# A state-space scan on one Trainium2 core: the skip term as a diagonal product in the sum over states, and the gate applied on VectorE

## The chip, the cores and the metric

The kernel runs on one core of one Trainium2 chip. The metric is the device time of one execution in microseconds; before the change it is 18559.42 us, the median of three runs (18539.3 to 18562.05).

## What is computed

Two layers over an image of 8 x 128 x 128 x 128 (batch, channels, height, width), both added to their input. The first is an attention layer in frequency and space; the change doesn't touch it. The second is a selective state-space layer (Mamba). Per batch the 16,384 pixels are a sequence of vectors of 128 channels; `W_in` makes 256 inner channels `xs` and 256 gate channels `z`. Cut to what matters:

```python
xc = silu(conv(xs))                       # 4 taps along the sequence
dt, Bm, Cm = split(xc @ W_xproj)          # 16 states
delta = softplus(dt @ W_dt + b_dt)
h = exp(delta * A) * h + (delta * xc) * Bm      # per step, inner channel and state
y = sum over states of h * Cm
y = y + xc * D_param                      # the skip term
y = y * silu(z)                           # the gate
out = y @ W_out
```

All of it is float32.

## The kernel before

The second layer is the scan part, the last section of `tile_kernel`. It takes the sequence in chunks of T = 512 pixels: 32 chunks for each of 8 batches, 256 cycles in all. The state space of a chunk has 256 inner channels x 16 states = 4,096 rows of 512 pixels. One step works on 2 x 128 of these rows, so a chunk has ST = 16 steps. Step s of chunk i does, each on its own engine:

- `product` (L1239, TensorE): delta * xc times Bm for the 256 rows, as 32 small products with diagonal matrices (`bd`), into the PSUM tile `hb` (two banks, two such tiles in turn). In the profile it is a run of 64 records `hb<-bd,duT`. It is issued one step ahead of its scan.
- `decay` (L1231, ScalarE): exp(delta * A), two tiles `dA`, three steps ahead.
- `scan` (L1254, VectorE): two `tensor_tensor_scan` instructions of 128x512 that run the recurrence along the pixels, `hs<-dA,state,hb`.
- `keep_state` (ScalarE): the last column, kept for the next chunk.
- `weigh` (L1268, GpSimd): times Cm, 128x1024, into `hc`.
- `add` (L1273, TensorE): the sum over states. Group g is the four steps 4g to 4g+3; each of their tiles is multiplied by `gath` (four identity matrices of 32 on top of each other), 32 output rows a product, and summed in the PSUM tile `y`. Groups 0 and 1 make the half h = 0 of the 256 channels, groups 2 and 3 the half h = 1. A product shows as two records.

Around these stands the work of once a chunk, spread over the steps by hand in the list `beside` (L1319): an entry (step, which chunk, function) says at which step it is issued, and for the chunk before (-1), this one (0), the next (1) or the one after (2). The convolution (`conv`, products `e_xc`), `gate` (`e_z`, then silu into `sz`), `xproj` (`e_x`), `step_sizes` (`e_dt`, then softplus into `dl`), `drive` (delta * xc), `turn` (transposes `e_t`), `diagonals` (the tiles `bd`, VectorE), `project` (the product with W_out, `e_o`) and `residual` are such entries. Each engine's instructions go through `InOrder` (L169), which keeps them in the order in which they are written: in step n `keep_state(n-1)`, `product(n+1)`, `first`, `decay(n+3)`, `scan(n)`, `beside`, `weigh(n)`.

The PSUM tiles are: two `hb` of two banks each, and four single banks, one tag each (`bank`, L1091). `y` has bank 3 to itself.

What the change touches is the end of a chunk's sum. `add(i, 0, ...)` in steps 5 and 6 and `add(i, 1, ...)` in step 10 sum the half h = 0; in step 11 `skip(i, 0)` (L1288) adds xc * D on VectorE, reading `y` from PSUM and writing `yt` in SBUF; in step 12 `gated(i, 0)` (L1297) multiplies `yt` by `sz` in place on GpSimd. The half h = 1 follows with `add(i, 2, ...)` in step 14, and in the next chunk `add(i, 3, ...)` in step 2, `skip` in step 3 and `gated` in step 4. `project` reads both halves of `yt` in step 8. `xc` is made by `conv_act` (L1105) in step 2 for the next chunk, in three buffers.

```python
dve.scalar_tensor_tensor(
    c["yt"][:, h, :], c["xc"][:, h, :], d_par[:, h : h + 1], c.pop(("y", h)), ALU.mult, ALU.add
)
```

Of the kernel before, what the change touches and what calls it, by code (L numbers as in the profile page):

```python
# [9 lines left out]
F32 = mybir.dt.float32  # L10
AF = mybir.ActivationFunctionType
ALU = mybir.AluOpType
# [15 lines left out]
T = 512  # L28
# [162 lines left out]
def tile_kernel(ctx: ExitStack, tc: tile.TileContext, I: dict, out: bass.AP):  # L191
    nc = tc.nc
# [23 lines left out]
    i = _CONSTS.index("group4")  # L216
# [48 lines left out]
    with tc.tile_pool(name="a_x", bufs=12) as xp_, tc.tile_pool(name="a_p", bufs=5) as pp_, tc.tile_pool(  # L265
        name="a_t", bufs=2
    ) as tp_, tc.tile_pool(name="a_s", bufs=2) as sp_, tc.tile_pool(name="a_ps", bufs=3, space=PSUM) as psum, tc.tile_pool(
        name="a_pg", bufs=2, space=PSUM
    ) as psumg:
        pe, dve, act, gps = (InOrder(tc, e) for e in (nc.tensor, nc.vector, nc.scalar, nc.gpsimd))  # L270
# [150 lines left out]
    with tc.tile_pool(name="b_x", bufs=1) as xp_, tc.tile_pool(name="b_g", bufs=2) as gp_, tc.tile_pool(  # L421
        name="b_w", bufs=2
    ) as wk, tc.tile_pool(name="b_s", bufs=1) as sp_, tc.tile_pool(name="b_ps", bufs=8, space=PSUM) as psum:
        pe, dve, act, gps = (InOrder(tc, e) for e in (nc.tensor, nc.vector, nc.scalar, nc.gpsimd))
# [21 lines left out]
        def bank(name):  # L446
            return psum.tile([128, 512], F32, name=name, tag="ps")
# [175 lines left out]
        def gated(n):  # L623
            b, g = divmod(n, NGR)
            qt, c0 = g // 4, 4 * (g % 4)
            e, o = (t.rearrange("p (c s) -> p c s", c=4) for t in live.pop(("x", n)))
            d = live["d", b, qt][:, c0 : c0 + 4, 1:64]
            out_, tmp = (wk.tile([128, 2, 4, 128], F32, name=n_, bufs=k) for n_, k in (("eo", 2), ("et", 1)))
            for j, t in enumerate((e, o)):
                a0 = live["g", b, qt, j][:, c0, 0:1]  # L630
                a = bass.AP(a0.tensor, a0.offset, [a0.ap[0], [NU, 4], [1, 2], [1, 64]])
                dve.tensor_tensor(
                    out_[:, j].rearrange("p c (t s) -> p c t s", t=2), t.rearrange("p c (t s) -> p c t s", t=2), a, ALU.mult
                )
            cs, sn = slice(1, 64), slice(64, 127)
            for to, at, frm, by in ((0, cs, o[:, :, sn], half), (0, sn, o[:, :, cs], mhalf),
                                    (1, cs, e[:, :, sn], mhalf), (1, sn, e[:, :, cs], half)):
                dve.scalar_tensor_tensor(tmp[:, to, :, at], d, by, frm, ALU.mult, ALU.mult)
            mid = [t.rearrange("p j c s -> p (j c) s")[:, :, 1:127] for t in (out_, tmp)]
            gps.tensor_tensor(mid[0], mid[0], mid[1], ALU.add)  # L640
            live["p", n] = out_
# [43 lines left out]
        for n in range(total + 3):  # L685
            b, g = divmod(n, NGR)
            if 0 <= n - 1 < total:
                fft_x(n - 1)
                gated(n - 1)
# [43 lines left out]
    with tc.tile_pool(name="c_w", bufs=1) as cw_, tc.tile_pool(name="c_qk", bufs=1) as qkp, tc.tile_pool(  # L733
        name="c_x", bufs=4
    ) as srcp, tc.tile_pool(name="c_v", bufs=8) as vp_, tc.tile_pool(name="c_s", bufs=2) as sp_, tc.tile_pool(
        name="c_ps", bufs=6, space=PSUM
# [8 lines left out]
        pe, dve, act, gps = (InOrder(tc, e) for e in (nc.tensor, nc.vector, nc.scalar, nc.gpsimd))  # L745
# [15 lines left out]
        def conv(n, o, r):  # L761

            b, cv, gq = order[n]
            if o == 0:
                banks[n, r] = psum.tile([128, 2, 256], F32, name="c_mm", tag="ps")
            grid = ahead[n].rearrange("p f (i j) -> p f i j", j=GR)
            rs = slice(32 * r, 32 * r + 32)
            for s in range(4):
                y0, x0 = 8 * s + o // 2, o % 2
                pe.matmul(  # L770
                    banks[n, r][32 * s : 32 * s + 32].rearrange("p f (i j) -> p f i j", j=32),
                    lhsT=taps[rs, gq, cv, o, :], rhs=grid[rs, :, y0 : y0 + 8, x0 : x0 + 32],
                    start=(o == 0), stop=(o == 3),
                )
            if o == 3:
                (use_q, use_k, use_v, use_v)[cv](b, cv, 4 * gq + r, banks.pop((n, r)))
                if r == 3:
                    ahead.pop(n)
                    load(n + 4)
# [107 lines left out]
    with tc.tile_pool(name="d_o", bufs=1) as op_, tc.tile_pool(name="d_v", bufs=2) as vp_, tc.tile_pool(  # L887
        name="d_k", bufs=2
    ) as kp, tc.tile_pool(
        name="d_w", bufs=3  # L890
    ) as wk, tc.tile_pool(name="d_s", bufs=1) as sp_, tc.tile_pool(name="d_pa", bufs=2, space=PSUM) as psa, tc.tile_pool(
        name="d_ps", bufs=4, space=PSUM
    ) as psum:
        pe, dve, act, gps = (InOrder(tc, e) for e in (nc.tensor, nc.vector, nc.scalar, nc.gpsimd))
# [130 lines left out]
    with tc.tile_pool(name="e_c", bufs=1) as cp, tc.tile_pool(name="e_w", bufs=2) as wk, tc.tile_pool(  # L1025
        name="e_h", bufs=4
    ) as hp, tc.tile_pool(name="e_d", bufs=3, space=DRAM) as dp, tc.tile_pool(
        name="e_b", bufs=2, space=PSUM
    ) as hbp, tc.tile_pool(name="e_g", bufs=1, space=PSUM) as psum:
        def fixed(name, shape, src):  # L1030
            t = cp.tile(shape, F32, name=name)
            nc.sync.dma_start(t if len(shape) == 2 else t.rearrange("p a b -> p (a b)"), src)
            return t
# [3 lines left out]
        unit = fixed("unit", [128, 128], I["consts"][:, 0:128])  # L1037
# [3 lines left out]
        wout = fixed("wout", [128, 2, C], I["wout"])  # L1041
        dv = fixed("dv", [128, 6], I["dvec"])
        conv_b, b_dt, d_par = dv[:, 0:2], dv[:, 2:4], dv[:, 4:6]
        A = fixed("A", [128, NM, NBK], I["alog"])
        nc.scalar.activation(A, A, AF.Exp)
        nc.vector.tensor_scalar(A, A, -1.0, None, ALU.mult)  # L1046

# [5 lines left out]
        ch = {}  # L1053
# [4 lines left out]
        pe, dve, act, gps = (InOrder(tc, e) for e in (nc.tensor, nc.vector, nc.scalar, nc.gpsimd))  # L1058
# [45 lines left out]

        def conv_act(i):  # L1105
            c = ch[i]
            c["xc"] = wk.tile([128, 2, T], F32, name="xc", bufs=3)
            for h in range(2):
                act.activation(c["xc"][:, h, :], c.pop(("xcp", h)), AF.Silu, bias=conv_b[:, h : h + 1])

# [68 lines left out]
        def turn_act(i, part):  # L1179
            c = ch[i]  # L1180
            if part == 0:
                c["duT"] = wk.tile([128, NTB, DI], F32, name="duT")
            act.copy(c["duT"][:, 2 * part : 2 * part + 2, :].rearrange("p j d -> p (j d)"), c.pop("tp"))
# [14 lines left out]
        def diagonals(i, mp, j):  # L1198


            c = ch[i]
            if (mp, j) in ((0, 0), (1, 0)):
                c["bd", mp] = wk.tile([128, NTB, NQ, ND, 2], F32, name="bd")
            to = [128, NQ, ND, 2]
            b = c["bp"][:, 32 * j : 32 * j + DS].rearrange("p (q m) -> p q m", m=NM)[:, :, 2 * mp : 2 * mp + 2]
            dve.tensor_tensor(
                c["bd", mp][:, j], same.unsqueeze(1).unsqueeze(3).to_broadcast(to), b.unsqueeze(2).to_broadcast(to), ALU.mult
            )
# [22 lines left out]
        def decay(n):  # L1231
            i, h, mp, k = where(n)
            for j in range(2):
                dA = hp.tile([128, T], F32, name="dA", bufs=10)
                kk = 4 * h + k
                act.activation(dA, ch[i]["dlr", h][:, k, :], AF.Exp, scale=A[:, 2 * mp + j, kk : kk + 1])
                dAs[n, j] = dA
# [35 lines left out]
        def add(i, g, *js):  # L1273

            if g % 2 == 0 and 0 in js:
                ch[i]["y", g // 2] = bank("y", 3)
            for j in js:
                for k in range(4):
                    pe.matmul(
                        ch[i]["y", g // 2][k * NR : (k + 1) * NR, :], lhsT=gath, rhs=hcs[ST * i + 4 * g + k][:, j, :],  # L1280
                        start=(g % 2 == 0 and j == 0), stop=(g % 2 == 1 and j == 1), skip_group_check=True,
                    )
            if 1 in js:
                for k in range(4):
                    del hcs[ST * i + 4 * g + k]


        def skip(i, h):  # L1288

            c = ch[i]  # L1290
            if h == 0:
                c["yt"] = wk.tile([128, 2, T], F32, name="yt", bufs=1)
            dve.scalar_tensor_tensor(
                c["yt"][:, h, :], c["xc"][:, h, :], d_par[:, h : h + 1], c.pop(("y", h)), ALU.mult, ALU.add
            )

        def gated(i, h):  # L1297
            yt = ch[i]["yt"][:, h, :]
            gps.tensor_tensor(yt, yt, ch[i]["sz"][:, h, :], ALU.mult)

        def project(i):
            c = ch[i]
# [4 lines left out]
        def residual(i):  # L1307
# [15 lines left out]
            (1, 1, lambda i: conv(i, 1, 3)),  # L1323
            (1, 0, lambda i: more_diagonals(i, range(11, 16))),
            (2, 1, conv_act),
            (2, -1, lambda i: add(i, 3, 0, 1)),
            (3, -1, lambda i: skip(i, 1)),
            (4, -1, lambda i: gated(i, 1)),
            (4, 1, xproj),
            (5, 1, xproj_act),  # L1330
            (5, 0, lambda i: add(i, 0, 0)),
            (6, 0, lambda i: add(i, 0, 1)),
            (6, 1, step_sizes),
            (6, 2, norm),
# [5 lines left out]
            (9, 1, lambda i: drive(i, 1)),  # L1340
            (9, 2, lambda i: conv(i, 0, 0)),
            (10, 0, lambda i: add(i, 1, 0, 1)),
            (11, 0, lambda i: skip(i, 0)),
            (11, 1, lambda i: diagonals(i, 0, 0)),
            (11, 1, lambda i: turn(i, 0)),
            (11, 2, lambda i: conv(i, 0, 1)),
            (12, 0, lambda i: gated(i, 0)),
            (12, 1, lambda i: turn_act(i, 0)),
            (12, 1, lambda i: diagonals(i, 0, 1)),
            (12, 2, lambda i: conv(i, 0, 2)),  # L1350
# [15 lines left out]
        for n in range(-2 * ST, (total + 1) * ST):  # L1366
            i, s = divmod(n, ST)
# [40 lines left out]
```

## Time and profile before

| what | value |
|---|---|
| median of three runs | 18559.42 us |
| the profiled execution | 18481.4 us, its span 18479.6 us |
| scan part | from about 6,600 us to the end |
| scans `hs`, VectorE | 7936 + 256, 1,269 and 1,206 ns each |
| products `hb`, TensorE | 262144 records, 4919.3 us busy |
| sum over states `y`, TensorE | 16384 records, 2053.4 us busy |
| `e_x`, `e_z`, `e_o`, TensorE | 1024 records each, 517.4, 522.6 and 509.5 us busy |
| `hc`, GpSimd | 4096, 2,377 ns each |
| skip, `yt<-xc,dv,y`, VectorE | 512, 731 ns each |
| gate, `yt<-yt,sz`, GpSimd | 512, about 1,279 ns each |

The times of a group of instructions are the union of its instructions (busy) and the mean length of one; lengths on TensorE overlap, since a product starts before the one ahead of it has left the array, so the distance between two starts tells more of its price than its length. In a timeline a row is a run of like instructions: start, length, engine, line, operation, output<-inputs, shapes, number of records, and in brackets the idle time of that engine before it with what ended it. Line L180 is the helper of `InOrder` through which nearly all instructions pass, so the tiles' names tell them apart.

### The profile page before, as it was taken

The page shows a single profiled execution, that of the slowest core. Times are in us where ns is not written, and L with a number is a line of the kernel's source. Part 1 is how long each engine was busy: PE and PEld are TensorE (multiplying, and loading weights), DVE is VectorE, ACT ScalarE, POOL GpSimd, SP SyncE. Part 2 cuts the span into 40 slices and gives each one's busy share as a digit, 9 for nine tenths or more (in the row PEclk, how much of TensorE's full clock was granted, in tenths as well). Part 3 has the DMA queues.
Part 4 walks back from the last instruction along what each step waited for, and adds up shares of the span by engine and source line. Part 5 has one row for each costly group of instructions (what it writes and reads, how often), then busy time and mean ns, then how long its engine had stood idle before and what let it go on. Part 6 is the DMA issues. An engine that isn't in the chain of part 4 may idle for free.

```text
span 18479.6 us, 790974 instructions
## 1 busy us (share of the span) xinstructions
PE 16503.3 (89%) x353336; PEld 9529.9 (52%) x353336; DVE 14244.2 (77%) x15987; ACT 12009.6 (65%) x26077; POOL 13090.9 (71%) x7572
## 2 busy tenths in 40 slices
PE   7789988888888889999999999999999999999998
PEld 5566665566555544444444444444444444444444
DVE  5544544334444479999999999999999999999999
ACT  4443434334233358778778878888888878887887
POOL 3333334444222269999999999999999989998998
PEclk8889999988999999999999999999999999999999
DMA  9963337777776654444454445444544454445443
GB/s 375 371 235 89 96 106 248 240 230 218 207 204 192 186 139 100 103 96 100 97 105 101 100 96 108 99 99 98 106 98 99 100 103 100 99 98 105 98 98 88
DMA packets 2434566, 2601.34 MB, mean 141 GB/s; under 512 B 1221965, under 2 KB 1624013, under 8 KB 2396866
## 3 DMA queue, kind: packets, MB, share of 16 engines
q1 hardware_dynamic: 1730850, 2206.28, 43.9%
q10 hardware_dynamic: 679840, 277.32, 7.1%
q0 software_dynamic: 20480, 67.13, 1.1%
q8 instruction: 2783, 45.60, 1.1%
q14 instruction: 613, 5.02, 0.1%
HBM read 1715.23 MB, written 834.93 MB: 138 GB/s over the span
## 4 chain that ended last, share of the span: by engine, by line
PE 56%; DVE 22%; DMA 8%; issue 7%; ACT 6%; POOL 1%; SPq 1%; DVEq 0%; ACTq 0%; POOLq 0%
DVE hs L180 15%; PE hb L180 14%; PE y L180 8%; PE c_mm L180 6%; PE e_xc L180 4%; DVE bd L180 3%; PE e_z L180 3%; PE e_x L180 3%; PE d_b L180 2%; PE a_mm L180 2%; DMA d_of<-OFL 2%; PE c_gram L180 2%; PE d_p L180 2%; DMA X<-d_x 2%; ACT L180 2%
## 5 line engine op out<-in xcount | busy, mean ns | idle before, releaser
L180 POOL TENSOR_TENSOR hc<-hs,crep 128x1024 f32<-128x1024 f32 x4096 | 9653.4, 2377 | 982.4 <-DVE hs L180 858.1
L180 DVE TENSOR_TENSOR_SCAN hs<-dA,state,hb 128x512 f32<-128x512 f32 x7936 | 9611.4, 1269 | 558.2 <-PE hb L180 418.8
L180 PEld LDWEIGHTS hb<-bd,duT 64*32 64x32 f32 x262144 | 3727.5, 106 | 3971.3 <-issue 2808.4
L180 PE MATMUL hb<-bd,duT 64*32 64x128 f32 x262144 | 4919.3, 275 | 798.9 <-issue 417.8
L180 ACT ACTIVATE dA<-dlrep,A 128x512 f32<-128x512 f32 x8192 | 5443.8, 714 | 59.6 <-DMA dlrep<-dld 51.6
L180 PE MATMUL e_xc<-u,wf 128*128 128x512 f32 x4096 | 2263.9, 646 | 34.1 <-DVE A L1046 20.8
L180 PE MATMUL y<-hc,gath 128*32 128x512 f32 x16384 | 2053.4, 601 | 32.5 <-issue 31.2
L180 ACT COPY state<-hs 128x2 f32<-128x2 f32 x4096 | 775.9, 189 | 1676.2 <-DVE hs L180 1649.5
L180 ACT ACT_TABLE_LOAD x1057 | 1356.1, 1283 | 75.0 <-PE e_dt L180 40.1
L180 PE MATMUL c_mm<-src,taps 32*32 32x512 f32 x32768 | 1211.5, 626 | 191.8 <-issue 158.7
L180 DVE COPY vst<-c_mm 128x512 f32<-128x512 f32 x1024 | 685.0, 689 | 717.4 <-PE c_mm L180 620.6
L180 ACT ACTIVATE bd<-same,bt 128x64 f32<-128x64 f32 x4096 | 1054.0, 339 | 0.8 <-PE hb L180 0.8
L180 DVE TENSOR_TENSOR bd<-same,e_bt 128x512 f32<-128x512 f32 x1536 | 1036.7, 675 | 0.0
L180 PEld LDWEIGHTS c_mm<-src,taps 32*32 32x32 f32 x32768 | 681.2, 105 | 683.7 <-issue 493.5
L180 POOL TENSOR_SCALAR qm<-vst,cst 128x512 f32<-128x512 f32 x256 | 505.4, 2070 | 745.4 <-DVE vst L180 745.2
L180 ACT ACTIVATE junk<-vst 128x256 f32<-128x256 f32 x1024 | 416.4, 410 | 923.0 <-DVE vst L180 921.9
L180 PE MATMUL a_mm<-xt,wp 128*128 128x256 f32 x3072 | 760.6, 409 | 264.5 <-ACT pk L180 184.1
L180 POOL TENSOR_TENSOR eo<-eo,et 128x1008 f32<-128x1008 f32 x128 | 298.8, 2334 | 969.3 <-DVE et L180 960.8
L180 POOL DMA_DIRECT2D X<-d_x x256 | 139.1, 543 | 1069.5 <-DVE d_x L180 939.9
L180 PEld LDWEIGHTS e_xc<-u,wf 128*128 128x128 f32 x4096 | 654.7, 194 | 440.2 <-issue 436.1
L180 DVE TENSOR_TENSOR d_x<-d_p,d_x 128x512 f32<-128x512 f32 x256 | 274.9, 1074 | 780.3 <-DMA d_x<-in_x 490.0
L180 PEld LDWEIGHTS a_mm<-xt,wp 128*128 128x128 f32 x3072 | 619.3, 205 | 421.7 <-ACT pk L180 194.6
(179 smaller groups left out, 20011.2 us busy)
## 6 DMA issues: line engine op xcount, KB each, us to landing
dlrep<-dld SPq DMA_DIRECT2D x2048, 256.0 KB
crep<-cd SPq DMA_DIRECT2D x2048, 128.0 KB
dld<-dl SPq DMA_DIRECT2D x256, 512.0 KB
src<-Pq SPq DMA_DIRECT2D x128, 544.5 KB
src<-Pv SPq DMA_DIRECT2D x128, 544.5 KB
src<-Pk SPq DMA_DIRECT2D x128, 544.5 KB
src<-Px SPq DMA_DIRECT2D x128, 544.5 KB
xt<-in_x SPq DMA_DIRECT2D x64, 1024.0 KB
```

The lines of the kernel that those rows point to most:

```text
L180: made = method(*args, **kwargs)
```

## The change

A matrix `dd` is made once: for each half a 128 x 128 diagonal matrix of D_param (VectorE multiplies the identity `unit` by the column of D). Where `add` takes a new bank for `y` (g = 0 in step 5, g = 2 in step 14), a product of `dd` with `xc` now opens the sum (`start=True`), 128 x 128 by 128 x 512 in float32; the products with `gath` all add to it. `skip` is gone. `gated` moves from GpSimd to VectorE and to `skip`'s places, steps 11 and 3: a `tensor_tensor` that multiplies `y`, read from PSUM, by `sz` into `yt`. `xc` has two buffers instead of three.

```diff
--- before.py
+++ after.py
@@ -1041,6 +1041,9 @@
         wout = fixed("wout", [128, 2, C], I["wout"])
         dv = fixed("dv", [128, 6], I["dvec"])
         conv_b, b_dt, d_par = dv[:, 0:2], dv[:, 2:4], dv[:, 4:6]
+        dd = cp.tile([128, 2, 128], F32, name="dd")
+        for h in range(2):
+            nc.vector.tensor_scalar(dd[:, h, :], unit, d_par[:, h : h + 1], None, ALU.mult)
         A = fixed("A", [128, NM, NBK], I["alog"])
         nc.scalar.activation(A, A, AF.Exp)
         nc.vector.tensor_scalar(A, A, -1.0, None, ALU.mult)
@@ -1104,7 +1107,7 @@
 
         def conv_act(i):
             c = ch[i]
-            c["xc"] = wk.tile([128, 2, T], F32, name="xc", bufs=3)
+            c["xc"] = wk.tile([128, 2, T], F32, name="xc", bufs=2)
             for h in range(2):
                 act.activation(c["xc"][:, h, :], c.pop(("xcp", h)), AF.Silu, bias=conv_b[:, h : h + 1])
 
@@ -1274,29 +1277,24 @@
 
             if g % 2 == 0 and 0 in js:
                 ch[i]["y", g // 2] = bank("y", 3)
+                pe.matmul(ch[i]["y", g // 2], lhsT=dd[:, g // 2, :], rhs=ch[i]["xc"][:, g // 2, :], start=True, stop=False, skip_group_check=True)
             for j in js:
                 for k in range(4):
                     pe.matmul(
                         ch[i]["y", g // 2][k * NR : (k + 1) * NR, :], lhsT=gath, rhs=hcs[ST * i + 4 * g + k][:, j, :],
-                        start=(g % 2 == 0 and j == 0), stop=(g % 2 == 1 and j == 1), skip_group_check=True,
+                        start=False, stop=(g % 2 == 1 and j == 1), skip_group_check=True,
                     )
             if 1 in js:
                 for k in range(4):
                     del hcs[ST * i + 4 * g + k]
 
 
-        def skip(i, h):
+        def gated(i, h):
 
             c = ch[i]
             if h == 0:
                 c["yt"] = wk.tile([128, 2, T], F32, name="yt", bufs=1)
-            dve.scalar_tensor_tensor(
-                c["yt"][:, h, :], c["xc"][:, h, :], d_par[:, h : h + 1], c.pop(("y", h)), ALU.mult, ALU.add
-            )
-
-        def gated(i, h):
-            yt = ch[i]["yt"][:, h, :]
-            gps.tensor_tensor(yt, yt, ch[i]["sz"][:, h, :], ALU.mult)
+            dve.tensor_tensor(c["yt"][:, h, :], c.pop(("y", h)), c["sz"][:, h, :], ALU.mult)
 
         def project(i):
             c = ch[i]
@@ -1324,8 +1322,7 @@
             (1, 0, lambda i: more_diagonals(i, range(11, 16))),
             (2, 1, conv_act),
             (2, -1, lambda i: add(i, 3, 0, 1)),
-            (3, -1, lambda i: skip(i, 1)),
-            (4, -1, lambda i: gated(i, 1)),
+            (3, -1, lambda i: gated(i, 1)),
             (4, 1, xproj),
             (5, 1, xproj_act),
             (5, 0, lambda i: add(i, 0, 0)),
@@ -1340,11 +1337,10 @@
             (9, 1, lambda i: drive(i, 1)),
             (9, 2, lambda i: conv(i, 0, 0)),
             (10, 0, lambda i: add(i, 1, 0, 1)),
-            (11, 0, lambda i: skip(i, 0)),
+            (11, 0, lambda i: gated(i, 0)),
             (11, 1, lambda i: diagonals(i, 0, 0)),
             (11, 1, lambda i: turn(i, 0)),
             (11, 2, lambda i: conv(i, 0, 1)),
-            (12, 0, lambda i: gated(i, 0)),
             (12, 1, lambda i: turn_act(i, 0)),
             (12, 1, lambda i: diagonals(i, 0, 1)),
             (12, 2, lambda i: conv(i, 0, 2)),
```

## The prediction

> **What bounds the kernel now.** I read the page's shares first, then the table of waits, then the engines' timelines over one cycle. The scan part runs from about 6,600 us to the end, in 256 cycles of 16 steps (32 scans each). From 8,000 to 18,300 us the groups hold 6901 + 224 scans, that is 222.6 cycles in 10,300 us: **46.3 us a cycle**. Page, part 1:
>
> ```profile
> PE 16503.3 (89%) x353336; PEld 9529.9 (52%) x353336; DVE 14244.2 (77%) x15987; ACT 12009.6 (65%) x26077; POOL 13090.9 (71%) x7572
> ```
>
> Over the whole span no engine looks full. In the scan part alone six windows of 1,000 us give VectorE 949, TensorE 920 and GpSimd 918 us of busy time per 1,000. Busy time can't choose between them; who waits for whom can. From the waits of 8,000 to 18,300 us (engine and tile, releaser: us in total, times, longest):
>
> ```profile
> DVE hs L180 <- PE hb L180: 388.2, 532, 4.5
> ...
> PE hb L180 <- issue: 372.4, 258, 4.4
> PE hb L180 <- DVE hs L180: 300.7, 470, 1.2
> ...
> DVE hs L180 <- POOL hc L180: 31.1, 48, 2.6
> ...
> DVE yt L180 <- PE y L180: 9.0, 7, 2.8
> ```
>
> The two engines hold each other: VectorE's scan waits for TensorE's product hb 388.2 us (1.74 a cycle), and TensorE waits for a scan to free one of the two hb buffers 300.7 us (1.35 a cycle). GpSimd holds the scan up for 0.14 us a cycle. So the question is where in the cycle each wait stands. VectorE in a cycle without disturbance (start, length, what, idle before):
>
> ```profile
> 9785.41 4.80 DVE L180 TENSOR_TENSOR_SCAN hs<-dA,state,hb 128x512 f32<-128x512 f32 x4 [0.55 <-PE hb L180]
> 9790.63 2.45 DVE L180 TENSOR_TENSOR_SCAN hs<-dA,state,hb 128x512 f32<-128x512 f32 x2 [0.43 <-PE hb L180]
> ...
> 9817.15 7.14 DVE L180 TENSOR_TENSOR_SCAN hs<-dA,state,hb 128x512 f32<-128x512 f32 x6
> 9824.20 0.73 DVE L180 SCALAR_TENSOR_TENSOR yt<-xc,dv,y 128x512 f32<-128x512 f32 x1
> ...
> 9830.00 2.45 DVE L180 TENSOR_TENSOR_SCAN hs<-dA,state,hb 128x512 f32<-128x512 f32 x2 [0.36 <-PE hb L180]
> ```
>
> I find the steps by what stands between the scans: the scans of steps 6 and 8 (9785.41 and 9790.63) wait for their products, and from step 8 on VectorE has no idle time until step 6 of the next cycle at 9830.00. The cycle is 44.6 us here. TensorE in the same cycle:
>
> ```profile
> 9774.87 1.44 PE L180 MATMUL hb<-bd,duT 64*32 64x128 f32 x64 [0.55 <-DVE hs L180]
> ...
> 9784.10 1.16 PE L180 MATMUL hb<-bd,duT 64*32 64x128 f32 x64
> 9785.18 1.06 PE L180 MATMUL y<-hc,gath 128*32 128x512 f32 x8
> ...
> 9805.05 1.18 PE L180 MATMUL hb<-bd,duT 64*32 64x128 f32 x64 [0.90 <-DVE hs L180]
> ...
> 9807.99 1.15 PE L180 MATMUL hb<-bd,duT 64*32 64x128 f32 x64 [0.32 <-DVE hs L180]
> 9809.06 1.92 PE L180 MATMUL y<-hc,gath 128*32 128x512 f32 x16
> ...
> 9819.75 1.15 PE L180 MATMUL hb<-bd,duT 64*32 64x128 f32 x64 [0.38 <-DVE hs L180]
> ```
>
> TensorE waits for VectorE ahead of the products for steps 14 (0.90), 15 (0.32) and 3 (0.55 at 9774.87, 0.38 at 9819.75), and nowhere from the product of step 3 to that of step 8. So a cycle has two owners: **TensorE from the product of step 3 to the scan of step 8, VectorE from there to the scan of step 1, whose end frees the buffer for product 3**.
>
> **The change, part by part.**
>
> *Two 128x512 float32 products a cycle (added, TensorE).* They read xc and dd, both long there, and the bank y, which the DVE reader of steps 3 and 11 has left, so they bring no wait. The nearest rows are the other full products. Two e_x (9826.77, next product at 9828.68) take 1.91 us; one e_xc alone between hb products (9795.41 to 9796.46) takes 1.05; so a second one in a row costs 0.86. The new one stands between an hb product and the y products, which pay an entry of their own (8 records take 1.00, 16 take 1.86, so 0.86 and an entry of 0.14). I take 0.95, between 0.86 and 1.05. The group's mean of 0.63 us a record, two records a product, would say 1.26, but records overlap, so I use starts.
>
> *Where they stand.* The first one opens y in step 5, in the timeline just ahead of the y products at 9785.18: behind product 6, ahead of products 7 and 8. The scan of step 8 already waits 0.43 us for product 8, and TensorE has no idle time before it: all 0.95 us are on the path. Behind it also stand e_dt and, over ACT's dl, e_o, all of which move together. The second opens y in step 14, ahead of the 16 records at 9809.06: behind product 15, ahead of products 0 to 3. Products 0 to 2 are ready ahead of their scans, about 1 us or more where I checked (product 2 ends at 9818.3, its scan starts near 9819.5), so the delay reaches product 3, where TensorE would have waited 0.38 to 0.55 us anyway. In a mean cycle I size that cover as the third share of TensorE's 1.35 us: 0.38 of 1.60 here. That gives 0.32; with 0.55 of 1.77 it gives 0.42. I take 0.38. What is left, 0.57 us, delays product 3, and from there TensorE owns the path. If that cover is gone (a cycle in which an "issue" stall has used it) the full 0.95 counts.
>
> *VectorE: scalar_tensor_tensor becomes tensor_tensor.* The old row is 731 ns (x512). The nearest row of the new kind, a product of a PSUM tile and an SBUF tile of 128x512 without strides, is eo<-x_e,g at 687 and eo<-x_o,g at 679 ns: about 48 ns less. The far end is d_x<-d_p,d_x, the same kind with strides, at 1,074 ns, +343 ns. I take -48, the access being plain. Only the one in step 11 lies where VectorE owns the path: -0.05 us a cycle (bound +0.34). The other, in step 3, lies beside TensorE's stretch and counts nothing either way. It still waits for the same last y product (9.0 us in all now) and for sz, long made.
>
> *GpSimd loses yt<-yt,sz.* 2 x 1.28 us a cycle of an engine that nobody on the path waits for: at most its 31.1 us of delays in the window, 36 us over 256 cycles. I take nothing, since with a later TensorE these waits are the first to be covered. What moves earlier, yt for e_o, is not what e_o waits for (ACT dl is, 0.48 us at 9792.41). At the very end one GpSimd product, 1.3 us, leaves the tail.
>
> *xc with two buffers instead of three.* conv_act of step 2 takes the buffer whose last reader is now the product of step 14, four steps before. No wait. Two small products that make dd, once: under 1 us.
>
> **Sum.** 0.95 + 0.95 - 0.38 - 0.05 = **+1.47 us a cycle**, times 256 = +376 us. The profiled execution took 18481.4 us (span 18479.6), 78 us under the median of 18559.42; I add the difference to the median: **18935 us**, 2.0% slower.
>
> **A rule that speaks against this.** The rows are the waits above: 388.2 us of scans waiting for hb. The Trainium skill's "Perfetto Trace Analysis", Identifying the Most-Contended Engine, says that matmul busy time is a poor measure of how full TensorE is, that the share of weight loads is a better one, and that the engine with the highest occupancy is to be relieved. By it TensorE with 48% of weight loads in the windows has room, VectorE with 95% is the bound, and the sum would be two times -0.05 a cycle, some 25 us faster. I go by the waits: they tell of order, not of room.
>
> **Rivals.**
> *A, TensorE has room (faster).* Both products vanish in TensorE's waits for VectorE, 1.35 us a cycle, and VectorE's 2 x 0.048 x 256 = 25 us and GpSimd's 36 us are won: 18559 - 61 = 18498. It would decide if a product took no more than some 0.4 us and stood ahead of product 14 or 3. For it: VectorE is the busier engine. Against: TensorE waits behind the place of the first one nowhere before scan 8, and scan 8 waits. 4%. Something between, within 37 us of no change: 5%.
> *B, the second product is wholly covered* by the lead of products 0 to 2 and the wait at 3: 0.95 - 0.05 = 0.90, 230 us, 18790; with 0.86 a product 18767. It needs 0.95 us of cover and I see 0.4. 14%.
> *C, nothing is covered*, as in cycles with an instruction stall (the 372.4 us of "issue"), and each costs 1.05: 2.10 x 256 = 538 us, 19097. With the gate at the strided row 87 us more. 15%.
> *Mine*, between: 0.86 a product and 0.42 covered gives 1.25 or 18879; 1.05 and 0.32 gives 1.73 or 19002. 62%.
>
> **How the numbers follow.** The likeliest case is 18935. The range takes in B and C to their ends: 18767 to 19100; left out are A, no change, and the strided gate on top of C. A change under 0.2% (37 us) is about what a measurement here can't tell from none: faster 0.04, same 0.05, slower 0.91.
>
> **What would show it.** Right: y<-xc,dd with about 0.95 us from its start to the next y; scans of step 8 waiting for hb about 1.4 us instead of 0.43; TensorE's wait ahead of product 3 gone, those ahead of 14 and 15 still there; yt<-y,sz near 0.68 us; GpSimd's busy time down by 655 us at no gain. Wrong: if scan 8 waits no longer than before, TensorE had room (A); if product 3 still waits, B; if yt<-y,sz takes over 1 us, VectorE's stretch grew too.

## The result, and the profile after

The changed kernel takes 18732.79 us (median of four runs, 18712.62 to 18763.44) against 18549.36 (four runs): ratio 1.0103, 95% interval 1.0082 to 1.0124. It is slower, by 183 us; 376 us had been forecast. Page of the changed kernel, part 1:

```profile
PE 16992.7 (91%) x354360; PEld 9665.1 (52%) x354360; DVE 14258.4 (76%) x15989; ACT 12015.9 (64%) x26077; POOL 12496.5 (67%) x7060
```

TensorE has 489 us more to do, GpSimd 594 us less (655 had been forecast), and VectorE as much as before. The waits of 8,000 to 18,300 us (engine and tile, releaser: us in total, times, longest):

```profile
POOL hc L180 <- DVE hs L180: 1408.0, 1883, 4.9
...
DVE hs L180 <- PE hb L180: 618.8, 827, 4.2
...
PE hb L180 <- issue: 320.1, 239, 3.8
PE hb L180 <- DVE hs L180: 224.0, 361, 1.1
```

The window holds 217.7 cycles now. VectorE waits 2.84 us a cycle for TensorE's products, where it was 1.74, and GpSimd's freed time has become waiting for VectorE (1408.0 us in the window, 733.0 before). VectorE through one undisturbed cycle after the change (start, length, what, idle before):

```profile
12187.30 2.45 DVE L180 TENSOR_TENSOR_SCAN hs<-dA,state,hb 128x512 f32<-128x512 f32 x2 [0.55 <-PE hb L180]
12190.44 2.45 DVE L180 TENSOR_TENSOR_SCAN hs<-dA,state,hb 128x512 f32<-128x512 f32 x2 [0.69 <-PE hb L180]
12193.58 2.45 DVE L180 TENSOR_TENSOR_SCAN hs<-dA,state,hb 128x512 f32<-128x512 f32 x2 [0.69 <-PE hb L180]
...
12204.23 0.65 DVE L180 TENSOR_TENSOR yt<-y,sz 128x512 f32<-128x512 f32 x1
...
12232.93 2.45 DVE L180 TENSOR_TENSOR_SCAN hs<-dA,state,hb 128x512 f32<-128x512 f32 x2 [0.42 <-PE hb L180]
```

From scan 6 to scan 6 it is 45.63 us, 1.04 more than before. Scan 6 waits about as it did; scans 7 and 8 wait 0.69 each, where scan 7 had not waited and scan 8 0.43. TensorE in the same cycle:

```profile
12187.08 1.13 PE L180 MATMUL y<-xc,dd 128*128 128x512 f32 x2
12188.13 1.06 PE L180 MATMUL y<-hc,gath 128*32 128x512 f32 x8
...
12207.98 1.35 PE L180 MATMUL hb<-bd,duT 64*32 64x128 f32 x64 [1.14 <-DVE hs L180]
...
12212.00 1.12 PE L180 MATMUL y<-xc,dd 128*128 128x512 f32 x2
12213.05 1.92 PE L180 MATMUL y<-hc,gath 128*32 128x512 f32 x16
...
12220.05 1.16 PE L180 MATMUL hb<-bd,duT 64*32 64x128 f32 x64
...
12222.69 1.15 PE L180 MATMUL hb<-bd,duT 64*32 64x128 f32 x64 [0.42 <-DVE hs L180]
```

Each diagonal product takes 1.05 us from its start to the next. The second one (12212.00) is followed by a product 3 that **still waits** 0.42 us for VectorE: the delay was swallowed. Why is in the old kernel, in a cycle without any stall in TensorE:

```profile
11372.23 1.15 PE L180 MATMUL hb<-bd,duT 64*32 64x128 f32 x64 [0.90 <-DVE hs L180]
...
11375.18 1.15 PE L180 MATMUL hb<-bd,duT 64*32 64x128 f32 x64 [0.35 <-DVE hs L180]
...
11384.00 1.15 PE L180 MATMUL hb<-bd,duT 64*32 64x128 f32 x64 [0.68 <-DVE hs L180]
...
11386.94 1.15 PE L180 MATMUL hb<-bd,duT 64*32 64x128 f32 x64 [0.74 <-DVE hs L180]
```

TensorE waits four times, not three: 0.68 us ahead of product 2 as well and 0.74 ahead of product 3, together 1.42 behind the second product's place. The cycle on which the prediction rested shows neither in full, because it held a stall at that very place (same kernel, a line of TensorE's timeline that the prediction left out):

```profile
9815.77 0.41 PE L180 MATMUL hb<-bd,duT 64*32 64x128 f32 x3 [0.61 <-issue]
```

### The profile page after: what moved, and what is told of

Its sections match the earlier page's. It is cut to its first block, busy times and chain, and to the rows that moved or that the text cites. A ratio compares the mean times of both kernels' runs of the same rounds, so it can differ in the third digit from the quotient of the medians.

```text
span 18761.7 us, 792254 instructions
## 1 busy us (share of the span) xinstructions
PE 16992.7 (91%) x354360; PEld 9665.1 (52%) x354360; DVE 14258.4 (76%) x15989; ACT 12015.9 (64%) x26077; POOL 12496.5 (67%) x7060
## 4 chain that ended last, share of the span: by engine, by line
PE 60%; DVE 22%; issue 8%; DMA 7%; ACT 2%; POOL 1%; SPq 0%; DVEq 0%; POOLq 0%; ACTq 0%
DVE hs L180 15%; PE hb L180 15%; PE y L180 10%; PE c_mm L180 6%; PE e_xc L180 5%; PE e_z L180 3%; PE e_x L180 3%; PE a_mm L180 2%; DVE bd L180 2%; PE d_b L180 2%; PE c_gram L180 2%; DMA d_of<-OFL 2%; PE d_p L180 2%; DMA X<-d_x 1%; PE d_a L180 1%
## 5 line engine op out<-in xcount | busy, mean ns | idle before, releaser
L180 PEld LDWEIGHTS y<-hc,gath 128*32 128x32 f32 x16384 | 404.6, 109 | 1041.2 <-issue 1005.8
```

The lines of the kernel that those rows point to most:

```text
L180: made = method(*args, **kwargs)
```

## The experiments

Theory after the result: the first product (step 5) stands in TensorE's stretch and costs all of its 1.06 us; the second (step 14) is covered by TensorE's waits ahead of products 2 and 3. Rival 1: both cost in part, and the lighter GpSimd and VectorE buy something back. Rival 2: it is the second that costs.

The table has every run. The ratio is to the kernel before, run beside it. "Cycle" is the 5th percentile of the cycles 20 to 249 of each profile, counted from the scans' starts, so a cycle that no stall makes longer. The waits, in us, are medians over the cycles of about that length in which TensorE has no "issue" stall. By "issue" the profile means idle time in which an engine waits for nothing that the profile shows; the last section says what ends it.

| kernel | median us | ratio, 95% interval | cycle | scans 6, 7, 8 wait | products 14, 15, 2, 3 wait |
|---|---|---|---|---|---|
| before | 18549 | | 44.57 | 0.36, 0, 0.43 | 0.91, 0.35, 0.66, 0.74 |
| the change | 18733 | 1.0103, 1.0082 to 1.0124 | 45.60 | 0.42, 0.69, 0.69 | 1.14, 0.35, 0, 0.42 |
| e_first_only | 18705 | 1.0103, 1.0087 to 1.0119 | 45.59 | 0.36, 0.69, 0.69 | 1.14, 0.35, 0.60, 0.74 |
| e_second_only | 18505 | 0.9986, 0.9975 to 0.9996 | 44.58 | 0.42, 0, 0.43 | 0.91, 0.35, 0, 0.42 |
| e_no_products | 18496 | 0.9989, 0.9976 to 1.0001 | 44.52 | 0.42, 0, 0.43 | 0.86, 0.35, 0.58, 0.74 |
| e_first_late | 18474 | 0.9979, 0.9970 to 0.9989 | 44.52 | 0.42, 0, 0.43 | 0, 0.20, 0, 0.42 |
| e_second_late | 18702 | 1.0102, 1.0086 to 1.0117 | 45.57 | 0.55, 0, 0.43 | 0, 0.20, 0.68, 0.74 |
| e_late_twice | 18573 | 1.0036, 1.0022 to 1.0050 | 44.90 | 0.55, 0, 0.43 | 0, 0.20, 0, 0 |
| e_sum_early | 18483 | 0.9984, 0.9974 to 0.9994 | 44.11 | 0, 0, 0 | 0, 0.13, 0, 0 |
| e_balanced | 18502 | 0.9995, 0.9985 to 1.0005 | 44.36 | 0, 0, 0 | 0, 0, 0, 0 |
| e_first_twice | 18918 | 1.0212, 1.0195 to 1.0228 | 46.44 | 0.42, 1.55, 0.69 | 1.12, 0.35, 0, 0.42 |
| e_three_xc | 18715 | 1.0104, 1.0086 to 1.0122 | 45.59 | 0.42, 0.69, 0.69 | 1.13, 0.34, 0, 0.42 |
| e_late_half | 18336 | 0.9896, 0.9880 to 0.9913 | 44.03 | 0.43, 0, 0 | 0, 0, 0, 0.12 |
| e_half_no_products | 18399 | 0.9937, 0.9924 to 0.9951 | 44.02 | 0.45, 0, 0 | 0.32, 0.35, 0.56, 0.57 |

### One half at a time

`e_first_only`, on the kernel before (`e_second_only` is the same for h = 1: g == 2, the gate in step 3):

```diff
+                if g // 2 == 0:
+                    pe.matmul(y, lhsT=dd[:, 0, :], rhs=xc[:, 0, :], start=True, stop=False, ...)
...
-                        start=(g % 2 == 0 and j == 0), stop=(g % 2 == 1 and j == 1), ...
+                        start=(g == 2 and j == 0), stop=(g % 2 == 1 and j == 1), ...
...
-            (11, 0, lambda i: skip(i, 0)),
+            (11, 0, lambda i: gated_v(i, 0)),
...
-            (12, 0, lambda i: gated(i, 0)),
```

> Only the half h = 0 is changed (its diagonal product opens y in step 5, its gate goes to VectorE in step 11); the half h = 1 keeps skip and GpSimd gate, xc keeps three buffers. Theory: the first product costs its whole 1.06 us a cycle and the change's whole loss is here: +150 to +230 us over before; the scans of steps 7 and 8 wait for hb about 0.7 us each. Rival 1 (both products cost in part, and the lighter GpSimd and VectorE buy something back): about half of the loss, +95 us. Rival 2 (the first is hidden, the second costs): 0.

> Only the half h = 1 is changed (its diagonal product opens y in step 14, its gate goes to VectorE in step 3); h = 0 keeps skip and GpSimd gate. Theory: TensorE waits some 1.2 to 1.4 us ahead of the products of steps 2 and 3 in a cycle without a stall, so the 1.06 us are covered: -20 to +30 us, scans 6 and 8 wait 0.4 us as before. Rival 1: +95 us. Rival 2: +190 us.

Ratios 1.0103 and 0.9986. The first half alone loses as much as the whole change; the second loses nothing and may gain a little. The waits of 8,000 to 18,300 us, `e_first_only`:

```profile
DVE hs L180 <- PE hb L180: 581.9, 728, 5.1
...
PE hb L180 <- issue: 345.4, 260, 3.7
PE hb L180 <- DVE hs L180: 336.2, 509, 1.6
```

and `e_second_only`:

```profile
DVE hs L180 <- PE hb L180: 430.2, 611, 5.2
...
PE hb L180 <- issue: 318.9, 243, 3.8
...
PE hb L180 <- DVE hs L180: 195.4, 327, 1.2
```

The first product goes into VectorE's waits (388.2 before, 581.9). The second goes into TensorE's own (300.7 before, 195.4), which nobody pays for. Both rivals fall.

### The change without its products

```diff
-                pe.matmul(ch[i]["y", g // 2], lhsT=dd[:, g // 2, :], rhs=..., start=True, ...)
...
-                        start=False, stop=(g % 2 == 1 and j == 1), ...
+                        start=(g % 2 == 0 and j == 0), stop=(g % 2 == 1 and j == 1), ...
```

> The change without its two products: the skip term is left out of the sum, the gate is on VectorE, GpSimd is relieved. Theory: only VectorE's 0.05 us in step 11 is won, -10 to -35 us. Rival 1 (relief buys back a good part of the products' cost): -100 us or more.

Ratio 0.9989 (0.9976 to 1.0001), some 20 us by the ratio, which the interval doesn't tell from no change, and 0.05 us in the cycle. GpSimd has 594 us less to do than before and VectorE 24 us less, and that buys next to nothing: VectorE's gate takes about 675 ns where skip took 731, and the scans hardly waited for GpSimd (31.1 us in the window before).

### The same products in other places

`e_first_late`, on the change: the first product moves into the sum, ahead of `add(1)` in step 10.

```diff
-                pe.matmul(... dd[:, g // 2, :] ..., start=True, ...)
+                if g == 2:
+                    diagonal(i, 1, True)
+            if g == 1 and 0 in js:
+                diagonal(i, 0, False)
...
-                        start=False, stop=(g % 2 == 1 and j == 1), ...
+                        start=(g == 0 and j == 0), stop=(g % 2 == 1 and j == 1), ...
```

> As the change, but the product of h = 0 is issued in step 10, inside the sum (ahead of add(1)), where VectorE owns the path and TensorE then waits 0.9 us ahead of product 14 and 0.3 ahead of product 15. Theory: the cost goes; -20 to +40 us against before, the wait ahead of 14 nearly gone, scans 6 and 8 back to 0.4 us, scan 7 to none. Rival 1: TensorE's work counts wherever it stands, +190 us as the change.

Ratio 0.9979: no loss is left, and it beats both kernels, by 39 us against the old one. TensorE's waits for VectorE, where it now stands:

```profile
PE hb L180 <- DVE hs L180: 49.9, 169, 0.5
```

300.7 before; product 14 no longer waits. As a counter-test `e_second_late` moves the second one into TensorE's stretch, ahead of `add(3)` in step 2 (in the lines above: `if g % 2 == 1 and 0 in js: diagonal(i, g // 2, False)`).

> As e_first_late, but the product of h = 1 stands in step 2, ahead of add(3) and behind the product of step 3, that is in TensorE's own stretch, instead of opening y in step 14. Same instructions, one moved. Theory: it is now on the path with its whole 1.06 us a cycle, +150 to +250 us over before (about 18,690 to 18,750), scan 6 waits over 1 us; the wait ahead of product 3 is back at 0.6 us. Rival (TensorE's products cost little wherever they stand, the loss belongs to step 5 for some other reason): as e_first_late, -40 us.

Ratio 1.0102. Instruction for instruction it is `e_first_late`, and the product that was free now costs 228 us. What decides is the place. (It does not show at scan 6 alone, as expected: of the 1.05 us that the cycle grows, the scans' waits hold 0.86, with 0.2 at scan 4 and 0.55 at scan 5, which had not waited, and 0.1 more at scan 6. With two buffers of xc `conv_act` of the same step has to let this product read first; TensorE doesn't wait for that, its products `e_x` behind it have no idle time before them.)

### How much cover, and one copy more

`e_late_twice` is `e_first_late` with `diagonal(i, 1, False)` after `diagonal(i, 1, True)`; `e_first_twice` is the change with the product of h = 0 issued twice.

> As e_first_late, but the opening product of h = 1 in step 14 is issued twice (the skip term of that half counts double). It measures the cover: behind one product TensorE still waits 0.37 us ahead of product 3 in a cycle without a stall, a second one in a row takes 0.86. If only that wait covers, +0.5 us a cycle, +125 us over e_first_late (+85 over before). If the instruction stalls of the other cycles cover too, as the first copy seemed to find, +60 to +100 over e_first_late. If the cover is unlimited, 0.

> As the change, but the opening product of h = 0 in step 5 is issued twice (the skip term of that half counts double). A second product in a row takes 0.86 us of TensorE. Theory: it stands in TensorE's stretch with no cover, so all of it counts: a clean cycle goes from 45.6 to 46.5 us, +160 to +220 us over the change (the lower end, if cycles with an instruction stall take less, as the medians of the change against its clean cycles hint). Rival (the loss is one for the place, say for the turn of the bank, and not per product): 0 over the change.

`e_late_twice`: 1.0036 for 0.9979, 106 us more by the ratios, near the first of the three cases. Its cycle takes 0.38 us more: 0.86 less the 0.42 that was left ahead of product 3 would be 0.44. So the cover at that place is 1.4 to 1.5 us in a cycle without a stall: 1.42 by the waits of the old kernel, 1.06 + 0.42 = 1.48 by `e_first_late`, 1.06 + 0.86 - 0.38 = 1.54 by this run. `e_first_twice`: 203 us over `e_three_xc`, run beside it, 0.85 in the cycle. There is no cover in step 5; VectorE shows it (scans 6, 7 and 8):

```profile
12205.09 2.45 DVE L180 TENSOR_TENSOR_SCAN hs<-dA,state,hb 128x512 f32<-128x512 f32 x2 [0.42 <-PE hb L180]
12209.09 2.45 DVE L180 TENSOR_TENSOR_SCAN hs<-dA,state,hb 128x512 f32<-128x512 f32 x2 [1.54 <-PE hb L180]
12212.23 2.45 DVE L180 TENSOR_TENSOR_SCAN hs<-dA,state,hb 128x512 f32<-128x512 f32 x2 [0.69 <-PE hb L180]
```

### Three buffers for xc

```diff
-            c["xc"] = wk.tile([128, 2, T], F32, name="xc", bufs=2)
+            c["xc"] = wk.tile([128, 2, T], F32, name="xc", bufs=3)
```

> The change with xc in three buffers, as before. Theory: the third buffer is never waited for, so the time is that of the change, 1.010 of before, within 30 us. Rival (the second-last reader now in step 14 holds conv_act of step 2): faster by 50 us or more. It also gives the change a second sample.

1.0104: the third buffer is not waited for.

### Moving other work the same way

The two owners suggest more. `e_sum_early` issues `add(3)` in step 1 instead of 2; `e_balanced` also moves half of group 0.

```diff
-            (2, -1, lambda i: add(i, 3, 0, 1)),
+            (1, -1, lambda i: add(i, 3, 0, 1)),
...
-            (6, 0, lambda i: add(i, 0, 1)),
+            (8, 0, lambda i: add(i, 0, 1)),
             (8, -1, project),
```

> As e_first_late, and the last group of the sum, add(3), is issued in step 1 instead of 2, ahead of the product of step 3. The theory of the two owners says that only the 0.37 us are won that TensorE still waited ahead of product 3: -60 to -95 us against e_first_late, with scan 3 now waiting some 0.5 us and scan 6 hardly. If TensorE were full anyway: 0.

> As e_sum_early, and half of group 0 (add(0, 1)) goes from step 6, TensorE's stretch, to step 8 ahead of project, where TensorE waited 0.48 us for ScalarE's dl; hc has eight buffers. Theory: the wait of scan 8 (0.43 us) goes too, -100 to -190 us against e_first_late, -140 to -230 against before. If the later products then come late for the scans of steps 10 to 12, half of that.

Both missed: 0.9984 and 0.9995, no better than `e_first_late`'s 0.9979. Their undisturbed cycles are shorter (44.11 and 44.36 for 44.52), but scan 3 now waits, 0.5 and 0.75 us in such cycles and about 1.2 in the mean of the others; in `e_first_late` it didn't. A likely reason, not tested by itself: product 3's lead had caught the stalls of steps 0 and 1, and with `add(3)` ahead of it that lead is gone. `e_late_half` keeps `add(3)` in step 2 and moves only `add(0, 1)`, with `hc` in eight buffers:

> As e_first_late, with add(0, 1) moved from step 6 to step 8 ahead of project (hc in eight buffers) and add(3) left in step 2. One term of TensorE's stretch, 1.0 us, goes from in front of the product of step 8 into VectorE's stretch, where TensorE waits 0.48 us for dl. Theory: scan 8's wait of 0.42 us goes in every cycle, scan 6's stays: -50 to -110 us against e_first_late. If other waits take its place, as in the two kernels that moved add(3) too: 0.

Ratio **0.9896** (0.9880 to 0.9913), the best of all, 1.0% under the old kernel. By the ratios that is 154 us under `e_first_late`, more than the 50 to 110 expected. The windows of 1,000 us give TensorE 964 and VectorE 955 us of busy time; the waits:

```profile
DVE hs L180 <- PE hb L180: 326.7, 420, 4.1
PE hb L180 <- issue: 216.5, 183, 3.8
```

Scan 8 waits no more. To see what of it is the move and what the products cost there, `e_half_no_products` leaves them out:

> As e_late_half, without the two diagonal products: the skip term is left out. It tells whether e_late_half's gain of about 200 us is the move of add(0, 1) alone, and what the two products cost there. If the move is all of it and the products are covered where they now stand: the time of e_late_half within 40 us, 0.988 to 0.991 of before. If TensorE, now busier than VectorE, pays for them in part: 50 to 250 us faster than e_late_half.

Ratio 0.9937: the move (with the eighth buffer of `hc`, which no run tried by itself) gains without the products too. But with them the kernel is neither as fast nor slower, as the two cases had it, it is **faster**, 0.9896. The waits of `e_half_no_products`:

```profile
PE hb L180 <- issue: 423.7, 331, 4.6
DVE hs L180 <- PE hb L180: 371.7, 433, 5.1
```

The undisturbed cycles are equal (44.02 and 44.03). What differs is how many there are. TensorE's "issue" stalls in the products hb are 423.7 us without the diagonal products and 216.5 with them, and TensorE has no stall at all in 17 of 229 cycles, against 99 with them. The clock that the profile shows as granted to TensorE differs too: in the same window it is at half speed for 314 us without the products and for 154 with them, and over whole executions it is 0.956 to 0.960 in the five runs without them, 0.963 to 0.966 in the four with them.

## Why the prediction was wrong

The sign was right, and so was the picture of the two owners. The size was not.

- **The step that failed: "In a mean cycle I size that cover as the third share of TensorE's 1.35 us [...] I take 0.38. What is left, 0.57 us, delays product 3".** Nothing is left: `e_second_only`, with the second product alone, takes 0.9986 of the old time. In a cycle without a stall the waits that cover are 1.42 us, since product 2 waits as well. The prediction's cycle held a stall of 0.61 us between product 1 and its end, which had eaten the wait ahead of product 2 and half of that ahead of product 3.
- **What the sum took to stay as it was: the stalls.** In the mean cycle half of the cover or more is not waiting for VectorE. Between the last record of product 15 and the start of product 3, where the second product comes in (means over 229 cycles, one profile each):

| us a cycle | before | e_second_only |
|---|---|---|
| the whole stretch | 11.28 | 11.11 |
| waits ahead of products 2 and 3 | 0.53 | 0.13 |
| "issue" stalls | 0.78 | 0.38 |
| granted clock at half speed | 0.69 | 0.17 |

The stretch holds a product of 1.06 us more and isn't longer. The waits gave 0.40 of it, so 0.38 was near the mean of the waits, by luck, as it was reckoned from one wait of a disturbed cycle. The stalls gave 0.40 more, and the clock was at half speed for 0.52 us less.

- **"If that cover is gone (a cycle in which an "issue" stall has used it) the full 0.95 counts": also wrong,** for the stall shrinks when the product is there. TensorE's idle time from the start of product 0 to that of product 1, mean over the same cycles: 0.70 us before and 0.71 in `e_first_only`, without a second product; 0.34 in `e_second_only` and 0.32 in `e_first_late`, with it; 0.11 in `e_late_twice`.
- The price of a product, 0.95: it is 1.056 (median of 256, in both places), the upper bound: it pays its own entry, and the y products behind it pay theirs.
- The first product wholly on the path: right in an undisturbed cycle (`e_first_only`, `e_first_twice`). I had the wait at scan 8 grow to 1.4 us; it came as 0.69 at scan 7 and 0.69 at scan 8, since scan 7's product is delayed too and had only 0.44 us of lead.
- VectorE's gate -0.05, GpSimd's relief nothing, two buffers of xc nothing: right (`e_no_products`, `e_three_xc`).
- Rival B named the true case, at 18790 or 18767. By the undisturbed cycle it gives 1.04 us, 266 us; the runs show 183. The two profiled executions lie 282 us apart, the first 68 us under its median and the second 31 over, so their cycle means overstate the change. By medians against kernels without a product on the path (18705 against 18505, 18715 against 18496) the first product costs 200 to 219 us, 0.78 to 0.86 a cycle. That this is less than 1.04 fits the stalls, which fall from 372.4 to 320.1 us in the window from the old kernel to the change, and the clock, at half speed for 290 us before and 215 after; no run separates what each is worth.
- Rival A fell. The Trainium skill's "Perfetto Trace Analysis", Identifying the Most-Contended Engine, would have had room on TensorE by its weight loads and a gain from relieving VectorE. Room there was (`e_first_late` takes both products for nothing), but not at step 5; and relieving VectorE gave 0.9989 (0.9976 to 1.0001), which can't be told from no change.

## What to carry to other kernels

When two engines hold each other in turn, an added instruction costs nearly its full time in the stretch that its engine owns (here 0.8 to 1.04 us of 1.06), and nothing in the other's, as long as the idle time there holds it: look at where it is issued before counting how busy the engine is. Measure that cover on several cycles, stall-free ones among them, since a cycle with a stall shows less than there is, and don't take the stalls for fixed: here they, and the clock, changed with what was issued between them. And a work list by hand can be moved: here one product into the other stretch took the whole loss away, and half a group of the old work, moved in the same way, made the kernel 1.0% faster than it had been.

## What the hardware showed unexpectedly

TensorE's "issue" stalls shrink when full products are put among the runs of small ones: 423.7 us to 216.5 in the window from `e_half_no_products` to `e_late_half`, and the kernel with more to compute is the faster one (0.9896 against 0.9937, intervals apart, each against the old kernel beside it).

The traces tell what ends these stalls. Part 3 of the old kernel's page has a DMA queue that carries instructions:

```profile
q8 instruction: 2783, 45.60, 1.1%
```

It brings one packet of 16,384 bytes for about 254 records of TensorE (weight loads and products). All 258 stalls of the old kernel's 372.4 us, all 183 of `e_late_half` and all 331 of `e_half_no_products` end 1.15 to 1.9 us after such a packet has landed. A moment taken at random lies so in 15% of cases, and so do 15% of the old kernel's waits that VectorE ended. So in these stalls TensorE waited for its instructions. That full products give the supply time to catch up, one giving 1.05 us for four instructions and an hb run 1.09 us for 128, fits, but is argued, not shown; no run took the stalls away by themselves.

A stall is followed by more. In the old kernel's window the granted clock drops to half 76 times, for 3.4 us or a multiple of it, and 70 of the drops begin within 4 us of the end of a stall of over 0.5 us; 10% of moments taken at random lie so. At half speed the 64 records of an hb run start within 1.54 us instead of 0.89. So a stall can cost more than its own length, and part of what `e_late_half` gains may be the clock; the runs don't separate the two.
